# A graph network in one planned instruction order: the planner's costs for TensorE's switches, score tiles by pairs, and new aims

## The chip, the cores and the metric

The kernel runs on one NeuronCore of one Trainium2 chip. The metric is the device time of one execution in microseconds (us). The engines are TensorE (PE; its weight loads are shown as PEld), VectorE (DVE), ScalarE (ACT), GpSimd (POOL) and SyncE (SP). Each takes its own instructions in the order in which the program lists them.

## The reference, cut to what matters

There are 16 graphs (the batches) of N = 1024 nodes with D = 256 features and an integer adjacency matrix each. All of it is fp32. Layer 0 is attention with 8 heads of 32, masked by the adjacency; layer 1 is two graph attentions and a feed-forward network.

```
# layer 0, per batch
q, k, v = heads(x @ Wq), heads(x @ Wk), heads(x @ Wv)
e = einsum('hqd,hkd->hqk', q, k);  e = where(e >= 0, e, 0.2 * e)
h = softmax(where(adj > 0, e, NEG), axis=-1) @ v
y = layernorm(h, g1, b1)
x = layernorm(concat([y, x]) @ Wffn.T, g2, b2) + x
# layer 1, per batch
def gat(h, W, a):
    Wh = h @ W
    e = leaky_relu(Wh @ a[:F] + (Wh @ a[F:]).T, 0.2)
    return softmax(where(adj > 0, e, NEG), axis=1) @ Wh
h = layernorm(x + gat(gat(x, W1, a1), W2, a2), g_ln1, b_ln1)
x = layernorm(h + relu(h @ w_ff1 + b_ff1) @ w_ff2 + b_ff2, g_ln2, b_ln2)
```

## The kernel before

**The planner.** The whole program is one stream of instructions whose order is worked out when it is built. Each piece of work is a Python generator, called a thread here. Before it emits an instruction it yields `on(PE=..., ACT=..., DVE=..., POOL=..., SP=...)`, the cost in ns of that instruction on the engine or engines that could do it; it can also `take` and `give` a buffer of a pool, `wait` for an event, `fire` one, `start` another thread or set its `aim`, a due time. The class `Order` keeps a clock for every engine. Of all threads that could start within a window of 300 ns of the earliest, the one with the earliest aim goes next; where a thread names two engines, the one that ends first takes it. So a wrong cost does no harm to a result: it only puts instructions into another order. On the chip the engines follow the order as it stands and wait for each other by semaphores.

`HOP` and `TAIL` are delays from one engine to the next, `SWITCH` a price for a change between two kinds of products on TensorE. Operations that are marked `shared` (DVE with two SBUF inputs, and the multiplication on POOL) are kept from overlapping by `port`, the time at which the other engine may start.

**The work of a batch.** Scores are made transposed, one tile of 128 keys by all 1024 queries: two matmuls of 512 columns (`all_scores`, L605), 64 tiles in a batch, in PSUM tiles of two banks of which there are two. A tile then goes through `weights`: ACT copies 0.2 times the scores (L621), DVE takes the maximum of the two (L623, which frees the PSUM tile), ACT the exponential (L626), POOL multiplies by the mask (L630). `all_values` takes the tiles two by two: products with v, 32 columns wide and called narrow (L645), and products with a column of -1 that sum the weights; for half of them DVE first adds two tiles (`add_pair`, L675). A narrow tile is four products of 256 columns, each in its own quarter of the array. After a head, `after_head` takes out the sums (`ho`) and divides.

When all heads of a batch are done, `rest` runs for it beside the scores of the next: layer norm and the product with `Wffn` (`rows_pair`, L771, L774), rows of the graph layer (L803), two graph attentions (`attend`, L856 and L859 on DVE, eight tiles each; products L894 and L919), a feed-forward network (L959, L987), with transposes on TensorE (L366, L695, L839, L947) between. `project` prepares the batch after: transposes of x (L366), masks (L433), q and k (L486) and v (L518). These products share three PSUM banks, the pool `misc`.

**What sets the order.** The aims are shares of `SLOT`, 253 us, counted from a batch's first score: `AIM` for steady batches, `EARLY` for the first. `graph0`, `graph1` and `graph_step` give those of `attend`, `qk0`, `qk1` and `qk_step` those of the projections. A score tile is due at a fixed pace and can't start earlier than `lead` paces ahead of it:

```
due = t0 + (h * NT + t) / 2 * pace(b)
yield aim(due, AIM["lead"] * PACE)
yield take("scores")
ps = psum.tile([P, N], FT, tag="scores", name="ps_s")
yield on(PE=471)
```

Row statistics (`stats`) are two instructions on DVE per row tile and then a logarithm and an exponential on ACT (L349, L351), which the planner counts as 98 ns each.

Of the kernel before, what the change touches and what calls it, by code (L numbers as in the profile page):

```python
# [27 lines left out]
BIG = float(2**100)  # L28
# [6 lines left out]
class Order:  # L35
# [5 lines left out]
    HOP = dict(PE=53.0, ACT=35.0, DVE=36.0, POOL=80.0, SP=60.0)  # L41
    TAIL = dict(PE=163.0, ACT=103.0, DVE=84.0, POOL=42.0, SP=0.0)
    WINDOW = 300.0
    SWITCH = 93.0

    STRETCH = 3413.0
    WORK = 0.43

    def __init__(self, **pools):
        self.clock = defaultdict(float)  # L50
        self.port = 0.0
        self.transfers = 0.0
        self.narrow = False
        self.stretch, self.done, self.half = 0, 0.0, True
        self.pools = {k: [(0.0, i) for i in range(n)] for k, n in pools.items()}
        self.slot = {}
        self.queues = defaultdict(list)
        self.events = {}
        self.waiting = defaultdict(list)
        self.active = []  # L60
        self.made = 0
        self.now = 0.0
        self.busy = defaultdict(float)
# [73 lines left out]
    def run(self):  # L137
        while self.active:
            could = []
            for th in self.active:  # L140
                costs, shared, delay, narrow = th["op"]
                best = None
                for engine, cost in costs.items():
                    ready = th["ready"] + self.HOP[engine]
                    if th.get("last", ())[:2] == (engine, th["ready"]):
                        ready -= self.HOP[engine] + self.TAIL[engine]
                    t = asked = max(self.clock[engine], ready)
                    if shared and engine in ("DVE", "POOL"):
                        t = max(t, self.port)
                    if best is None or t + cost < best[0] + best[2]:  # L150
                        best = t, engine, cost, asked
                could.append((best, th))
            first = min(c[0][0] for c in could)
            (t, engine, cost, asked), th = min((c for c in could if c[0][0] <= first + self.WINDOW),
                                        key=lambda c: (c[1]["aim"], c[1]["no"]))
            if th["op"][1] and engine in ("DVE", "POOL"):

                before = [c for c in could if c[1]["op"][1] and c[0][1] in ("DVE", "POOL")
                          and c[0][1] != engine and c[0][3] < asked]
                if before:  # L160
                    (t, engine, cost, asked), th = min(before, key=lambda c: (c[1]["aim"], c[1]["no"]))
            costs, shared, delay, narrow = th["op"]
            self.active.remove(th)
            if engine == "PE":
                if narrow != self.narrow:
                    cost += self.SWITCH
                self.narrow = narrow
            end = self.clock[engine] = self.end(engine, t, cost)
            self.busy[engine] += cost
            if shared and engine in ("DVE", "POOL"):  # L170
                self.port = end
            self.now = t
            th["ready"] = end + self.TAIL[engine]
            th["last"] = engine, th["ready"]
            if delay:
                self.transfers = max(self.transfers, end + 1000) + 1450 * max(1, round(cost / 500))
                th["ready"] = max(end + delay, self.transfers + 1200)
                th["last"] = None, 0
            self.step(th, engine)
        stuck = {k: len(v) for k, v in list(self.waiting.items()) + list(self.queues.items()) if v}  # L180
        assert not stuck, f"threads that never end: {stuck}"


def on(shared=False, delay=0.0, narrow=False, **costs):
    return "on", (costs, shared, delay, narrow)


def pause(time):
# [11 lines left out]
def take(pool):  # L200
    return "take", pool
# [10 lines left out]
def aim(time, lead):  # L212
    return "aim", (time, lead)
# [17 lines left out]
def unshifted_path(  # L231
# [26 lines left out]
    PACE = SLOT / (H * NT // 2)  # L258


    AIM = dict(mask0=0.759, x=0.5882, x_step=0.0012, mask=0.7438, mask_step=0.0264, qk0=0.6333, qk1=0.7649,
               qk_step=0.0231, v0=0.863, v1=0.9566, v_step=0.0513, rows=-0.1328, rows_step=0.0338, first0=0.1095,
               first1=0.2264, graph0=0.0576, graph1=0.273, graph_step=0.0015, second=0.3518, second_step=0.0609,
               normed=0.8572, normed_step=0.058, ff_wait=(None, 0, 1, 0), ff=(0.6792, -0.0871, 0.5781, 0.4984),
               ff_step=0.0581, fast0=0.4431, fast1=0.9245, fast15=0.6119, lead=1.5024)

    EARLY = dict(x=0.87, x_step=0.0004, mask=0.7193, mask_step=0.0345, qk0=0.7893, qk1=0.9441, qk_step=0.0345,
                 v0=0.8496, v1=0.9733, v_step=0.0532, rows=-0.139, rows_step=-0.0236, first0=0.1365,
                 first1=-0.0311, graph0=-0.195, graph1=-0.027, graph_step=0, second=0.3474, second_step=0.0327,
                 normed=0.781, normed_step=0.02, ff_wait=(None, 0, 1, 0), ff=(0.633, 0.0209, 0.488, 0.493),  # L270
                 ff_step=0.0422)

    const = ctx.enter_context(tc.tile_pool(name="const", bufs=1))
# [8 lines left out]
    def share(b, name):  # L282
        return (EARLY if b < 2 else AIM)[name]

# [52 lines left out]
    def stats(srcs):  # L337

        n = len(srcs)
        mv = small.tile([P, n, 2], FT, name=f"mv{n}")  # L340
        for i, src in enumerate(srcs):
            st = small.tile([P, 6], FT, name="st")
            yield on(DVE=430)
            nc.vector.bn_stats(st, src)
            yield on(DVE=99)
            nc.vector.bn_aggr(mv[:, i, :], st)
        rs = small.tile([P, n], FT, name=f"rs{n}")
        yield on(ACT=98)
        nc.scalar.activation(rs, mv[:, :, 1], AF.Ln, bias=eps)  # L349
        yield on(ACT=98)  # L350
        nc.scalar.activation(rs, rs, AF.Exp, scale=-0.5)  # L351
        return mv, rs

# [231 lines left out]
    def pace(b):  # L585
        return PACE * {0: AIM["fast0"], 1: AIM["fast1"], B - 1: AIM["fast15"]}.get(b, 1.0)

    def all_scores():
        for b in range(B):
            yield wait(("stack", b, 0))  # L590
            t0 = begin[b] = work.now
            if b + 1 < B:
                yield start(project(b + 1, t0), t0)
            for h in range(H):
                yield wait(("stack", b, h))
                q, kk = stacks[b, h]
                for t in range(NT):
                    due = t0 + (h * NT + t) / 2 * pace(b)
                    yield aim(due, AIM["lead"] * PACE)
                    yield take("scores")  # L600
                    ps = psum.tile([P, N], FT, tag="scores", name="ps_s")
                    yield on(PE=471)
                    for nh in range(NH):
                        cols = slice(nh * HALF, (nh + 1) * HALF)
                        nc.tensor.matmul(ps[:, cols], kk[:, t * P:(t + 1) * P], q[:, cols], start=True, stop=True)  # L605
# [27 lines left out]
    def all_values():  # L633
        for b in range(B):
            for h in range(H):
# [13 lines left out]
                for d in range(0, NT, GV):  # L649
                    last, adds = d + GV == NT, d < ADDED * GV  # L650
                    for t in range(d, d + GV):
                        yield wait(("p", b, h, t))
                    if added:
                        yield wait(("p added", b, h, d - GV))
                    yield aim(begin[b] + (h * NT + d + 2) / 2 * pace(b), SLOT)
                    ps = [probs.pop((b, h, t)) for t in range(d, d + GV)]
                    for t, p in zip(range(d, d + GV), ps):
                        yield on(PE=430, narrow=True)
                        product(v[:, t, c:c + DH], p, 0, t == 0, False)
                        yield aim(begin[b], BIG)  # L660
                    if adds:
                        yield start(add_pair(b, h, d, ps), begin[b] + (h * NT + d + 2) / 2 * pace(b))
                    for p in added if adds else added + ps:
                        yield on(PE=430, narrow=True)
# [799 lines left out]
```

## Time and profile before

| | |
|---|---|
| median of 3 runs | 4434.45 us (4430.11 to 4434.94) |
| profiled execution | 4435.77 us, span 4433.9 us |
| busy, share of the span | PE 96%, PEld 70%, DVE 79%, ACT 68%, POOL 53% |
| mean clock granted to TensorE | 0.99 |
| scores, L605 | 2048 matmuls, 684.7 us busy |
| narrow products, L645 | 8192 and 6144 records, 559.2 and 407.9 us |
| maximum, L623 | 1024 on DVE, mean 1215 ns |
| mask, L630 | 1024 on POOL, mean 2332 ns |
| `attend`, L856 and L859 | 256 each on DVE, means 1446 and 1343 ns |
| logarithm, L349; exponential, L351 | 224 each on ACT, medians 296 and about 200 ns |

The span is the time from the first to the last instruction that the profiler saw. Busy times of TensorE overlap, since matmuls are pipelined; the distance from one start to the next says more. A number in square brackets in a timeline is idle time of that engine before the instruction, and the name behind it what ended it.

### The profile page before, as it was taken

What the parts mean: (1) busy time and instruction counts of PE and PEld (TensorE: products, weight loads), DVE (VectorE), ACT (ScalarE), POOL (GpSimd) and SP (SyncE); (2) the same over time, 40 slices, a digit from 0 to 9 for tenths busy, and PEclk for the clock granted to TensorE, in tenths of its full rate; (3) what the DMA queues carried; (4) which work ended last, traced back from release to release, by engine and by line L of the source; (5) the groups of instructions that cost most, each with busy time, mean ns of one, the idle gap of its engine ahead of it and who ended that gap; (6) DMA issues with size and microseconds to landing.
All of it is one profiled execution on the core that took longest, in us unless ns stands there. A gap on an engine that the chain in (4) does not pass through costs nothing.

```text
span 4433.9 us, 77232 instructions
## 1 busy us (share of the span) xinstructions
PE 4267.4 (96%) x30539; PEld 3082.5 (70%) x30539; DVE 3515.0 (79%) x5493; ACT 3004.8 (68%) x4488; POOL 2364.4 (53%) x1033
## 2 busy tenths in 40 slices
PE   8888999999999999999999999999999999999899
PEld 4455667677676776767777676776767777677687
DVE  6877878888788888888878788887788878788853
ACT  6656675676867667676676867667676676867632
POOL 5746464464736536473564736537464564736600
PEclk9999999999999999999999999999999999999999
DMA  5413223232222322222232222322323232221100
GB/s 181 124 53 87 74 72 87 70 93 70 87 79 70 93 67 83 83 83 82 65 95 73 86 79 70 94 67 77 84 81 88 63 96 74 86 79 41 34 20 20
DMA packets 156286, 344.86 MB, mean 78 GB/s; under 512 B 21750, under 2 KB 24332, under 8 KB 155916
## 3 DMA queue, kind: packets, MB, share of 16 engines
q1 hardware_dynamic: 112140, 260.13, 20.5%
q10 hardware_dynamic: 43776, 79.71, 6.3%
q8 instruction: 243, 3.98, 0.4%
q14 instruction: 127, 1.04, 0.1%
HBM read 239.09 MB, written 100.66 MB: 77 GB/s over the span
## 4 chain that ended last, share of the span: by engine, by line
PE 67%; DVE 28%; ACT 3%; issue 2%; POOL 0%; DMA 0%; ACTq 0%; SPq 0%; DVEq 0%; POOLq 0%
PE ps_a L645 15%; PE ps_s L605 10%; PE ps_m L894 9%; PE ps_m L919 8%; DVE att L856 7%; DVE att L859 6%; DVE p L623 5%; PE ps_m L959 4%; PE ps_m L486 4%; PE ps_m L987 3%; PE ps_m L771 3%; PE ps_m L803 2%; PE ps_m L774 2%; ACT p L621 2%; PE ps_m L366 1%
## 5 line engine op out<-in xcount | busy, mean ns | idle before, releaser
L630 POOL TENSOR_TENSOR p<-p,mask 128x1024 f32<-128x1024 f32 x1024 | 2363.6, 2332 | 1837.8 <-ACT p L626 1338.2
L623 DVE TENSOR_TENSOR p<-p,ps_s 128x1024 f32<-128x1024 f32 x1024 | 1220.1, 1215 | 344.5 <-ACT p L621 336.6
L626 ACT ACTIVATE p<-p 128x1024 f32<-128x1024 f32 x1024 | 1082.2, 1059 | 301.1 <-DVE p L623 256.4
L621 ACT ACTIVATE p<-ps_s 128x1024 f32<-128x1024 f32 x1006 | 996.0, 1020 | 198.2 <-PE ps_s L605 91.9
L605 PE MATMUL ps_s<-qs,ks 128*128 128x512 f32 x2048 | 684.7, 439 | 50.6 <-DVE p L623 46.6
L645 PE MATMUL ps_a<-p,v 128*32 128x256 f32 x8192 | 559.2, 388 | 12.2 <-POOL p L630 12.2
L605 PEld LDWEIGHTS ps_s<-qs,ks 128*128 128x128 f32 x2048 | 337.1, 190 | 276.2 <-issue 116.5
L894 PE MATMUL ps_m<-y,att 128*128 128x258 f32 x2048 | 484.6, 382 | 5.5 <-ACT y L864 1.9
L919 PE MATMUL ps_m<-y,att 128*128 128x256 f32 x2048 | 480.9, 381 | 1.8 <-ACT y L864 1.8
L959 PE MATMUL ps_m<-rT,wf 128*128 128x256 f32 x2048 | 472.6, 381 | 7.1 <-ACT z L324 2.4
L987 PE MATMUL ps_m<-wf,hid 128*128 128x256 f32 x2048 | 473.8, 380 | 1.3 <-ACT xT L324 1.1
L894 PEld LDWEIGHTS ps_m<-y,att 128*128 128x128 f32 x2048 | 386.4, 190 | 76.7 <-ACT hid L968 6.1
L645 PE MATMUL ps_a<-p,minus_ones 128*32 128x256 f32 x6144 | 407.9, 383 | 31.8 <-DVE p L675 31.5
L959 PEld LDWEIGHTS ps_m<-rT,wf 128*128 128x128 f32 x2048 | 379.6, 190 | 69.8 <-ACT hid L968 8.1
L987 PEld LDWEIGHTS ps_m<-wf,hid 128*128 128x128 f32 x2048 | 379.3, 190 | 59.1 <-issue 7.6
L919 PEld LDWEIGHTS ps_m<-y,att 128*128 128x128 f32 x2048 | 379.7, 190 | 55.8 <-ACT y L864 2.6
L645 PEld LDWEIGHTS ps_a<-p,v 128*32 128x32 f32 x8192 | 213.4, 109 | 288.7 <-issue 155.2
L675 DVE TENSOR_TENSOR p<-p 128x1024 f32<-128x1024 f32 x256 | 374.1, 1461 | 18.2 <-PE ps_a L645 16.8
L856 DVE SCALAR_TENSOR_TENSOR att<-first,second 128x1024 f32<-128x1024 f32 x256 | 370.1, 1446 | 13.5 <-ACT first L843 13.5
L859 DVE SCALAR_TENSOR_TENSOR att<-mask,att 128x1024 f32<-128x1024 fp8e4 x256 | 343.8, 1343 | 7.7
L645 PEld LDWEIGHTS ps_a<-p,minus_ones 128*32 128x32 f32 x6144 | 199.0, 111 | 172.4 <-DVE p L675 41.3
L864 ACT ACTIVATE y<-y,check 128x258 f32<-128x258 f32 x256 | 130.6, 510 | 247.6 <-DVE check L862 246.4
(106 smaller groups left out, 4427.8 us busy)
## 6 DMA issues: line engine op xcount, KB each, us to landing
qs<-qk_halves SPq DMA_DIRECT2D x256, 256.0 KB, 3.7
ks<-qk_halves SPq DMA_DIRECT2D x256, 256.0 KB, 5.1
adj_i<-in_adj_dram ACTq DMA_DIRECT2D x240, 256.0 KB, 3.2
qk_halves<-high SPq DMA_DIRECT2D x128, 256.0 KB, 2.5
qk_halves<-low SPq DMA_DIRECT2D x128, 256.0 KB, 2.9
xr<-in_x_dram ACTq DMA_DIRECT2D x64, 256.0 KB, 3.0
x_kept<-x SPq DMA_DIRECT2D x64, 256.0 KB, 2.1
x<-x_kept SPq DMA_DIRECT2D x64, 256.0 KB, 3.2
```

The costliest lines, as they stand in the source:

```text
L605: nc.tensor.matmul(ps[:, cols], kk[:, t * P:(t + 1) * P], q[:, cols], start=True, stop=True)
L621: nc.scalar.activation(p, ps, AF.Copy, scale=ALPHA)
L623: nc.vector.tensor_tensor(p, p, ps, op=OP.max)
L626: nc.scalar.activation(p, p, AF.Exp)
L630: nc.gpsimd.tensor_tensor(p, p, mask_of(b, t), op=OP.mult)
L645: nc.tensor.matmul(acc[i * DH:(i + 1) * DH, at:at + QN], w, p[:, i * QN:(i + 1) * QN], start=first, stop=last)
L856: nc.vector.scalar_tensor_tensor(e, first[:, 0, :], second[:, j:j + 1], first[:, 1, :], op0=OP.mult, op1=OP.max)
L859: nc.vector.scalar_tensor_tensor(e, mask_of(b, j), -1.0, e, op0=OP.mult, op1=OP.mult, accum_out=sums[:, j:j + 1])
L894: nc.tensor.matmul(pa[:, cols:cols + width], big[:, j, i * P:(i + 1) * P], rows[:, j, :width], start=(j == 0), stop=(j == NT - 1))
L919: nc.tensor.matmul(pa[:, i * D:(i + 1) * D], big[:, j, t * P:(t + 1) * P], y2[:, j, :D], start=(j == 0), stop=False)
L959: nc.tensor.matmul(pa[:, i * 2 * P:(i + 1) * 2 * P], wf1[:, dc, hc * P:(hc + 1) * P], rT[:, dc, :], start=(dc == 0), stop=(dc == DC - 1))
L987: nc.tensor.matmul(pa[:, i * D:(i + 1) * D], hid[hc // 2][:, hc % 2, i * P:(i + 1) * P], wf2[:, hc, :], start=(hc == 0), stop=False)
```

## The change

The planner's model gets new figures, and the order is worked out anew.

- The price of a switch on TensorE depends on what comes from and what goes to: `SWITCH` is a table over `narrow`, `single` (scores) and other products. A score tile costs 464 instead of 471.
- The shared port is kept for DVE and POOL apart: after a DVE operation POOL may start 54 ns before its end, after one on POOL DVE 130 ns before its end.
- The logarithm and the exponential of `stats` cost 318 and 105 ns.
- From batch 1 on, scores go by pairs of key tiles: at an even tile the thread takes both PSUM tiles of the pool, and the odd tile follows without a due time of its own.
- `AIM` and `EARLY` have new values.

The instructions themselves are the same but for the engine that takes a result out of PSUM, where the planner has the choice.

```
-    SWITCH = 93.0
+    SWITCH = {(None, "narrow"): 93.0, ("single", "narrow"): 93.0, ("narrow", None): 93.0,
+              ("narrow", "single"): 197.0, (None, "single"): 84.0}
...
-        self.port = 0.0
+        self.port = dict(DVE=0.0, POOL=0.0)
-        self.narrow = False
+        self.mode = None
...
                     if shared and engine in ("DVE", "POOL"):
-                        t = max(t, self.port)
+                        t = max(t, self.port[engine])
...
             if engine == "PE":
-                if narrow != self.narrow:
-                    cost += self.SWITCH
-                self.narrow = narrow
+                cost += self.SWITCH.get((self.mode, mode), 0.0)
+                self.mode = mode
...
             if shared and engine in ("DVE", "POOL"):
-                self.port = end
+                if engine == "DVE":
+                    self.port["POOL"] = end - 54.0
+                else:
+                    self.port["DVE"] = end - 130.0
...
-    AIM = dict(mask0=0.759, x=0.5882, x_step=0.0012, mask=0.7438, mask_step=0.0264, qk0=0.6333, qk1=0.7649,
-               qk_step=0.0231, v0=0.863, v1=0.9566, v_step=0.0513, rows=-0.1328, rows_step=0.0338, first0=0.1095,
-               first1=0.2264, graph0=0.0576, graph1=0.273, graph_step=0.0015, second=0.3518, second_step=0.0609,
-               normed=0.8572, normed_step=0.058, ff_wait=(None, 0, 1, 0), ff=(0.6792, -0.0871, 0.5781, 0.4984),
-               ff_step=0.0581, fast0=0.4431, fast1=0.9245, fast15=0.6119, lead=1.5024)
+    AIM = dict(mask0=0.7454, x=0.7836, x_step=0.0012, mask=0.7416, mask_step=0.0241, qk0=0.8169, qk1=0.7629,
+               qk_step=0.0234, v0=0.8897, v1=0.9566, v_step=0.0513, rows=-0.1328, rows_step=0.039, first0=0.1101,
+               first1=0.2264, graph0=-0.041, graph1=0.3629, graph_step=0.0128, second=0.3518, second_step=0.0609,
+               normed=0.8572, normed_step=0.058, ff_wait=(None, 0, 1, 0), ff=(0.6792, -0.0021, 0.5781, 0.4984),
+               ff_step=0.0549, fast0=0.4291, fast1=0.9756, fast15=0.6646, lead=1.5024)
...
-    EARLY = dict(x=0.87, x_step=0.0004, mask=0.7193, mask_step=0.0345, qk0=0.7893, qk1=0.9441, qk_step=0.0345,
+    EARLY = dict(x=0.9697, x_step=0.0004, mask=0.7306, mask_step=0.0331, qk0=0.7893, qk1=0.9441, qk_step=0.026,
...
-                 first1=-0.0311, graph0=-0.195, graph1=-0.027, graph_step=0, second=0.3474, second_step=0.0327,
+                 first1=-0.0311, graph0=-0.0903, graph1=-0.027, graph_step=0, second=0.3474, second_step=0.0327,
...
-        yield on(ACT=98)
+        yield on(ACT=318)
         nc.scalar.activation(rs, mv[:, :, 1], AF.Ln, bias=eps)
-        yield on(ACT=98)
+        yield on(ACT=105)
         nc.scalar.activation(rs, rs, AF.Exp, scale=-0.5)
...
-                    yield aim(due, AIM["lead"] * PACE)
-                    yield take("scores")
+                    if b == 0 or t % 2 == 0:
+                        yield aim(due, AIM["lead"] * PACE)
+                        for _ in range(2 if b else 1):
+                            yield take("scores")
+                    else:
+                        yield aim(t0, BIG)
                     ps = psum.tile([P, N], FT, tag="scores", name="ps_s")
-                    yield on(PE=471)
+                    yield on(PE=464, mode="single")
...
-                        yield on(PE=430, narrow=True)
+                        yield on(PE=430, mode="narrow")
```

More of the change, by code (lines that the diff above doesn't have):

```diff
@@ L140, in run @@
             for th in self.active:
-                costs, shared, delay, narrow = th["op"]
+                costs, shared, delay, mode = th["op"]
                 best = None
@@ L161, in run @@
                     (t, engine, cost, asked), th = min(before, key=lambda c: (c[1]["aim"], c[1]["no"]))
-            costs, shared, delay, narrow = th["op"]
+            costs, shared, delay, mode = th["op"]
             self.active.remove(th)
             if engine == "PE":
-                if narrow != self.narrow:
-                    cost += self.SWITCH
-                self.narrow = narrow
+                cost += self.SWITCH.get((self.mode, mode), 0.0)
+                self.mode = mode
             end = self.clock[engine] = self.end(engine, t, cost)
@@ L181, in run, with on @@
         assert not stuck, f"threads that never end: {stuck}"
-def on(shared=False, delay=0.0, narrow=False, **costs):
-    return "on", (costs, shared, delay, narrow)
+def on(shared=False, delay=0.0, mode=None, **costs):
+    return "on", (costs, shared, delay, mode)
 def pause(time):
@@ L258, in unshifted_path @@
     PACE = SLOT / (H * NT // 2)
-    AIM = dict(mask0=0.759, x=0.5882, x_step=0.0012, mask=0.7438, mask_step=0.0264, qk0=0.6333, qk1=0.7649,
-               qk_step=0.0231, v0=0.863, v1=0.9566, v_step=0.0513, rows=-0.1328, rows_step=0.0338, first0=0.1095,
-               first1=0.2264, graph0=0.0576, graph1=0.273, graph_step=0.0015, second=0.3518, second_step=0.0609,
-               normed=0.8572, normed_step=0.058, ff_wait=(None, 0, 1, 0), ff=(0.6792, -0.0871, 0.5781, 0.4984),
-               ff_step=0.0581, fast0=0.4431, fast1=0.9245, fast15=0.6119, lead=1.5024)
-    EARLY = dict(x=0.87, x_step=0.0004, mask=0.7193, mask_step=0.0345, qk0=0.7893, qk1=0.9441, qk_step=0.0345,
-                 v0=0.8496, v1=0.9733, v_step=0.0532, rows=-0.139, rows_step=-0.0236, first0=0.1365,
-                 first1=-0.0311, graph0=-0.195, graph1=-0.027, graph_step=0, second=0.3474, second_step=0.0327,
-                 normed=0.781, normed_step=0.02, ff_wait=(None, 0, 1, 0), ff=(0.633, 0.0209, 0.488, 0.493),
+    AIM = dict(mask0=0.7454, x=0.7836, x_step=0.0012, mask=0.7416, mask_step=0.0241, qk0=0.8169, qk1=0.7629,
[4 more added lines that the diff above has]
+    EARLY = dict(x=0.9697, x_step=0.0004, mask=0.7306, mask_step=0.0331, qk0=0.7893, qk1=0.9441, qk_step=0.026,
+                 v0=0.8496, v1=0.9733, v_step=0.0532, rows=-0.1833, rows_step=-0.0236, first0=0.1365,
+                 first1=-0.0311, graph0=-0.0903, graph1=-0.027, graph_step=0, second=0.3474, second_step=0.0327,
+                 normed=0.781, normed_step=0.02, ff_wait=(None, 0, 1, 0), ff=(0.6698, 0.0209, 0.488, 0.4266),
                  ff_step=0.0422)
@@ L663, in all_values @@
                     for p in added if adds else added + ps:
-                        yield on(PE=430, narrow=True)
+                        yield on(PE=430, mode="narrow")
                         product(minus_ones, p, QN, False, last and p is ps[-1])
```

## The prediction

> **What bounds the kernel now.** I read the page from the top, then asked where TensorE waits, then compared stretches of one batch.
>
> ```profile
> span 4433.9 us, 77232 instructions
> ...
> PE 4267.4 (96%) x30539; PEld 3082.5 (70%) x30539; DVE 3515.0 (79%) x5493; ACT 3004.8 (68%) x4488; POOL 2364.4 (53%) x1033
> ...
> PEclk9999999999999999999999999999999999999999
> ```
>
> TensorE is the bound, the clock is full nearly everywhere, and a busy TensorE is not one at its peak. So I measured its work by the distances from start to start in its timeline, taking the undisturbed ones as the cost. A 256-wide fp32 pass takes 0.216 us, a score tile (two matmuls) 0.464, a tile of narrow products (L645, eight records) 0.431. A narrow run costs 0.231 more than its tiles, in and out together, and a score tile right behind it 0.106 more again; behind other products a score tile costs nothing extra (0.680 from a 256-wide start to the instruction after the tile, less 0.216, is 0.464). With 515 narrow runs, 331 of them followed by scores, this makes 4124.6 us of work. The other 309 us of the span are stalls. From the first score of a batch to that of the next it is 266.8 us in the steady batches (5 to 14): 257.1 of work, 9.7 of stall.
>
> ```profile
> 1955.28 1.07 PE L645 MATMUL ps_a<-p,v 128*32 128x256 f32 x16
> 1956.17 0.61 PE L645 MATMUL ps_a<-p,minus_ones 128*32 128x256 f32 x8
> 1956.71 1.20 PE L605 MATMUL ps_s<-qs,ks 128*128 128x512 f32 x4
> 1957.75 1.90 PE L894 MATMUL ps_m<-y,att 128*128 128x258 f32 x8
> ...
> 1880.44 1.99 PE L987 MATMUL ps_m<-wf,hid 128*128 128x256 f32 x8
> 1882.90 0.70 PE L605 MATMUL ps_s<-qs,ks 128*128 128x512 f32 x2 [0.47 <-DVE p L623]
> 1883.94 0.73 PE L605 MATMUL ps_s<-qs,ks 128*128 128x512 f32 x2 [0.34 <-DVE p L623]
> ```
>
> The first four lines are a clean stretch: a pair of score tiles takes 1.04 us, 0.93 and the step out of narrow mode. In the last three, 2.46 us lie between the start of eight passes, worth 1.73, and the tile behind them, and the two tiles stand 1.04 us apart instead of 0.46: both wait for VectorE to free a score bank.
>
> ```profile
> 1815.00:1915.00 100.00, 97.36 (x654) 74.22 (x652) 86.20 (x161) 66.64 (x124) 34.19 (x16) 1.00 0.21 61
> 1915.00:2081.00 166.00, 165.03 (x1254) 116.70 (x1250) 131.02 (x181) 122.50 (x158) 111.44 (x49) 1.00 0.32 91
> ```
>
> The columns after the length are busy us of PE, PEld, DVE, ACT and POOL. Most of the stall lies in the first 100 us of a batch, where DVE is busiest. By what follows it, a steady batch stalls 4.9 us before or within score tiles, 4.8 among other products, 0.3 in narrow runs.
>
> ```profile
> 1894.46 1.25 DVE L856 SCALAR_TENSOR_TENSOR att<-first,second 128x1024 f32<-128x1024 f32 x1
> 1895.74 1.22 DVE L859 SCALAR_TENSOR_TENSOR att<-mask,att 128x1024 f32<-128x1024 fp8e4 x1
> ...
> 1828.75 0.30 ACT L349 ACTIVATE rs<-mv,eps 128x2 f32<-128x2 f32 x1
> 1829.07 0.20 ACT L351 ACTIVATE rs<-rs 128x2 f32<-128x2 f32 x1
> 1829.18 1.01 ACT L621 ACTIVATE p<-ps_s 128x1024 f32<-128x1024 f32 x1
> ...
> PE ps_s L605 <- DVE p L623: 46.6, 84, 1.9
> PE ps_a L645 <- DVE p L675: 31.5, 5, 9.5
> ```
>
> DVE runs `attend` (L856, L859) seven or eight tiles in a row, 2.6 us each; the score stalls sit around these two blocks, and behind one of them a product waits up to 9.5 us (last line, from TensorE's waits). The ACT lines show the pair Ln, Exp at a pitch of 0.32 and 0.11 us, where the planner has 98 ns each.
>
> **What the Trainium skill says.** "TensorEngine Tiling (Array Packing)", Key Properties: a change of tiling mode drains TensorE. The trace agrees: other to narrow and narrow to other are 0.093 us longer each. "TensorE: Matmul & The Clock Gate", the section on the 32x32 sub-arrays: ACT and DVE are strict FIFO; so a maximum (L623) behind eight `attend` tiles waits for all of them, as here. "SBUF — State Buffer", section "SBUF: two separate sides": DVE with two SBUF inputs and GpSimd lock each other out of a shared port for a whole instruction. The trace agrees: L856 is 1.25 us alone and 3.13 beside L630 at 1887.06. The new port rule lets the second start slightly before the first ends.
>
> **The change, part by part.** No product, size or buffer changes; the built programs have the same number of matmuls, POOL operations and DMA issues. What changes is the order on every queue and which engine evacuates: 32 instructions go from ACT to DVE, 28 of them `ho` (0.58 us on ACT, 0.69 on DVE), some 1.3 us more DVE in a batch. I price that at nothing: DVE has 49 us free in a steady batch, and ACT loses as much.
>
> *Switches.* Counted in both orders and priced as above: narrow runs go from 32 to 35 in a steady batch (+3 x 0.231 = +0.69 us), score runs behind narrow ones from 20 to 14 (-6 x 0.106 = -0.64). Over the kernel it is 515 to 547 and 331 to 252: +7.4 - 8.4 = **-1 us**. The model's 84 ns for other-to-score, which the trace doesn't show, makes the planner pay in narrow runs for nothing.
>
> *Loads.* The new aims move the q and k projections, and with them the DMAs on SP, as well as the issues of `xr` and masks on ACT. By TensorE's work the last projection stands 87 us ahead of the next batch's first score, where it was 81; writing and reading back take 2.9 and 5.1 us from issue to landing (rows of the DMA issues), and the queues are 20 and 6% busy. Cost nothing; without that cover it would be those 8 us a batch.
>
> *Pairs.* From batch 1 on both score banks must be free before a pair is issued, and pairs go from 350 to 485. In a steady batch the TensorE work between the ends of tile k-2 and the start of tile k is at least 4.1 us, where it was 2.4. What a pair needs: 0.46 and 0.2 to ACT, two copies (L621) at 0.90, the second maximum 1.13, hops 0.3, 3.9 us from its start, 3.0 in the measure above. So pairs alone cause no wait. Yet large slack did not prevent stalls before: tiles with 30 us of slack waited 0.4 to 0.6 us, behind the `attend` blocks.
>
> *Blocks.* The longest DVE work between two maxima falls from 26.7 and 25.1 us to 19.0 and 14.9 (sums of pitches in the DVE order), to 0.65 of it. I scale the score stall with that: 4.9 to 3.2, **-1.7** a batch (bounds: 0 and -4.9).
>
> *ACT and port figures.* 14 groups of Ln and Exp in a batch, each counted 0.227 us too short (0.423 new, 0.196 old), put ACT 3.2 us behind plan in a batch. Work placed to be just in time came late. Of the 4.8 us among other products I take a third, **-1.6** (bounds: +1, since new neighbours bring new misses, and -3.2). What is late next: the transposes behind `y` and `hT` (L366), whose chain through statistics stays as long.
>
> So a steady batch gains 3.3 us; with batches 4 to 14, eleven: **-36**. *Batches 1 to 3 and 15.* Batch 1 has stalls of 9.9 us at 274.9 and 383.8, behind blocks of 27.9 and 19.4 us that become 18.2 and 17.5: half of the 9.7 and 1.9 that go, -6. Batches 2 and 3 as the steady ones, -7. Batch 15: 9.9 us at 4160.9 behind a block that goes from 17.8 to 11.7, -3. Together **-16** (bounds: +10 and -35; their aims moved most, and the trace has no other order to compare). Batch 0 keeps single tiles: 0.
>
> The sum is -1 - 36 - 16 = -53 against the profiled execution's 4435.8 us (span 4433.9, 1.9 around it), thus **4382 us**; the median shown, 4434.45, is 1.3 lower.
>
> **Rivals.** *Nearly all stalls behind DVE go*: 4.9 + 2.4 in eleven batches is 80, with 25 at the ends: 4330. For it: the middle of each batch shows no stall, so the order can be that good. Against it: `attend` is still 20 us of DVE twice a batch. *The stalls only move*: TensorE reaches the next late operand sooner, and the 4.8 us grow by what the scores save; only a part of the ends is won: 4430. For it: DVE is busy 86 of 100 us where it matters, and gets more. *Slower: pairs crowd the evacuations.* Two copies and two maxima stand together on ACT and DVE, so one of the three `misc` banks is freed later and the product for it stalls everything behind it on TensorE. A batch has 32 pairs; from 3.3/32 = 0.10 us per pair this eats the gain, and at 0.20 us, with the ends' gain lost too, it is 36 us slower: 4472. For it: ACT evacuations of 0.47 to 0.58 us already wait behind L621 and L626. Against it: the clean middle is made of pairs already. That the pairing is not in effect is excluded: the new order shows 485 pairs.
>
> **How the numbers follow.** Some 8.9 us (0.2%) is what a measurement of this kernel can tell from no change. Moderate gain 0.52 (own range 4355 to 4420), nearly all 0.18, stalls move 0.16, slower 0.14. Of the third, more than half is within 0.2%. Faster 0.77, same 0.09, slower 0.14. The range 4335 to 4445 leaves out the worse half of the slower case and the tail of the best.
>
> **What would show it.** A steady batch near 263.5 us instead of 266.8; TensorE's wait of L612 for the maximum (now L630) down by a third; no 9.9 us wait behind L682; TensorE's work still near 4124 us. A batch as long as before with fewer score waits would prove the second rival, longer waits of products for ACT or DVE the third. Steady batches below 261 us would mean that I undersized the blocks.

## The result, and the profile after

The new kernel takes **4402.17 us** (median of 6 runs, 4396.82 to 4403.73); the kernel before takes 4434.41 us beside it (4430.11 to 4435.19). The ratio is 0.9926, with an interval of 0.9913 to 0.9938: 0.74% faster, 32 us. The profiled execution took 4397.53 us; its span is 38.2 us shorter.

The head of the page of the new kernel:

```profile
span 4395.7 us, 77297 instructions
...
PE 4246.0 (97%) x30539; PEld 3077.3 (70%) x30539; DVE 3543.5 (81%) x5525; ACT 2979.7 (68%) x4456; POOL 2418.1 (55%) x1033
...
PEclk9999999999999999999999999999999999999999
```

The matmuls are as many as before, at the same clock. TensorE is busy 21 us less although it does the same products: its overlapping busy time is no measure of work. Priced from start to start, as in the prediction, its work is 4123.6 us after 4124.6. So the gain is stall that went. The first score of each batch gives the stretches (us):

| stretch | before | after | change |
|---|---|---|---|
| to the first score | 38.6 | 37.1 | -1.5 |
| batches 0 to 3 | 977.5 | 967.0 | -10.5 |
| batches 4 to 14 | 2933.4 | 2906.7 | -26.7 |
| batch 15, to the last score | 246.6 | 252.1 | +5.5 |
| after the last score | 237.8 | 232.8 | -5.0 |

A steady batch now takes 264.3 us instead of 266.8, with 7.2 of stall instead of 9.7. Where in the batch the stall lies depends on how it is counted. The prediction says that its split (4.9, 4.8, 0.3) goes by what follows the stall. Its figures come out of the trace in another way: a stall behind a score tile or a narrow run, in front of another product, is in them counted with the tile or the run ahead of it. Counted by the matmul that comes late, the split is different. All these are estimates from the distances from start to start, good to some 0.3 us:

| stall of a steady batch, us | before, as the prediction counts | after, same count | before, by the matmul that comes late | after, same count |
|---|---|---|---|---|
| score tiles | 4.9 | 2.4 | 3.9 | 0.6 |
| other products | 4.8 | 3.7 | 5.5 | 6.3 |
| narrow products | 0.3 | 1.1 | 0.3 | 0.3 |

Below, the split is by the matmul that comes late. Scores have lost 3.3 us of stall, and other products have gained 0.8.

The two stretches of one batch of the new kernel (columns as in the prediction: length, then busy us of PE, PEld, DVE, ACT and POOL):

```profile
1795.00:1895.00 100.00, 98.23 (x654) 75.78 (x656) 84.93 (x169) 67.70 (x122) 35.04 (x16) 1.00 0.20 57
1895.00:2059.00 164.00, 163.04 (x1253) 115.02 (x1246) 135.39 (x176) 118.52 (x158) 114.31 (x49) 1.00 0.33 95
```

With the same 654 products, TensorE is idle 1.8 us in the first stretch where it was 2.6; the loss stays in the part where `attend` runs, and is smaller. TensorE's waits from 1300 to 3600 us, some nine steady batches, name it (what it waited for: us in total, times, longest). Before:

```profile
PE ps_s L605 <- DVE p L623: 12.4, 35, 0.5
PE ps_m L366 <- DVE y L360: 4.7, 9, 0.5
PE ps_m L771 <- ACT mask L437: 3.6, 9, 0.4
PE ps_m L959 <- ACT z L324: 2.1, 9, 0.2
PE ps_m L366 <- ACT hT L385: 1.5, 9, 0.2
PE ps_m L695 <- DVE rT L383: 1.5, 8, 0.2
```

After:

```profile
PE ps_m L369 <- DVE rT L386: 6.7, 8, 0.9
PE ps_m L966 <- ACT z L327: 6.4, 9, 0.7
PE ps_m L994 <- DVE hn L709: 5.9, 9, 0.7
PE ps_m L846 <- ACT first L850: 2.2, 9, 0.2
PE ps_m L436 <- DVE rT L386: 0.8, 5, 0.2
PE ps_s L612 <- DVE p L630: 0.7, 1, 0.7
PE ps_m L846 <- DVE low L494: 0.3, 1, 0.3
```

The waits of scores for the maximum have all but gone from the steady part (12.4 to 0.7 us). Those of other products have grown from 13.4 to 22.3 us; the three longest of them come about once a batch each. In the new list every one is a wait for a bank of `misc`: the instruction named behind the arrow takes a result out of such a bank and is no operand of the product. Before, that for `y` was a wait for an operand; the other four, 8.7 us, were for a bank too. This view counts only idle time that it can put down to a semaphore, so it shows less than the distances do. Over the whole span of the new kernel:

```profile
PE ps_s L612 <- DVE p L630: 35.3, 36, 4.9
PE ps_a L652 <- DVE p L682: 25.2, 11, 9.5
```

Of the 35.3 us, 0.7 lie in the window above; before it was 12.4 of 46.6. Outside the window the score waits are as large as ever, 34.6 after 34.2. And the wait behind `add_pair` (now L682) is still there: 25.2 us after 31.5.

The chain of work that ended last says the same from the other side, by engine. Before, then after:

```profile
PE 67%; DVE 28%; ACT 3%; issue 2%; POOL 0%; DMA 0%; ACTq 0%; SPq 0%; DVEq 0%; POOLq 0%
```
```profile
PE 81%; DVE 14%; ACT 3%; issue 2%; POOL 0%; DMA 0%; ACTq 0%; SPq 0%; DVEq 0%; POOLq 0%
```

DVE's share of the chain has halved, while its busy time has grown by 28 us.

### The profile page after: what moved, and what is told of

The parts are those of the page before. It is cut to its first block, busy times and chain, and to the rows that moved or that the text cites. A ratio compares the mean times of both kernels' runs of the same rounds, so it can differ in the third digit from the quotient of the medians.

```text
span 4395.7 us, 77297 instructions
## 1 busy us (share of the span) xinstructions
PE 4246.0 (97%) x30539; PEld 3077.3 (70%) x30539; DVE 3543.5 (81%) x5525; ACT 2979.7 (68%) x4456; POOL 2418.1 (55%) x1033
## 4 chain that ended last, share of the span: by engine, by line
PE 81%; DVE 14%; ACT 3%; issue 2%; POOL 0%; DMA 0%; ACTq 0%; SPq 0%; DVEq 0%; POOLq 0%
PE ps_a L652 16%; PE ps_m L901 10%; PE ps_s L612 9%; PE ps_m L926 9%; PE ps_m L994 8%; PE ps_m L966 8%; DVE p L630 4%; PE ps_m L489 4%; PE ps_m L810 3%; DVE att L863 3%; PE ps_m L778 3%; PE ps_m L781 2%; DVE att L866 2%; PE ps_m L369 2%; PE ps_m L521 2%
## 5 line engine op out<-in xcount | busy, mean ns | idle before, releaser
L637 POOL TENSOR_TENSOR p<-p,mask 128x1024 f32<-128x1024 f32 x1024 | 2417.3, 2377 | 1752.1 <-ACT p L633 1401.4
L612 PE MATMUL ps_s<-qs,ks 128*128 128x512 f32 x2048 | 639.1, 430 | 35.5 <-DVE p L630 35.3
L612 PEld LDWEIGHTS ps_s<-qs,ks 128*128 128x128 f32 x2048 | 350.0, 190 | 213.5 <-issue 68.0
L966 PE MATMUL ps_m<-rT,wf 128*128 128x256 f32 x2048 | 472.7, 381 | 13.2 <-ACT z L327 7.3
L966 PEld LDWEIGHTS ps_m<-rT,wf 128*128 128x128 f32 x2048 | 380.6, 190 | 81.8 <-issue 11.0
L652 PE MATMUL ps_a<-p,minus_ones 128*32 128x256 f32 x6144 | 408.7, 384 | 25.2 <-DVE p L682 25.2
L682 DVE TENSOR_TENSOR p<-p 128x1024 f32<-128x1024 f32 x256 | 385.4, 1506 | 25.7 <-PE ps_a L652 25.6
L863 DVE SCALAR_TENSOR_TENSOR att<-first,second 128x1024 f32<-128x1024 f32 x256 | 393.7, 1538 | 4.5 <-ACT first L850 4.5
L866 DVE SCALAR_TENSOR_TENSOR att<-mask,att 128x1024 f32<-128x1024 fp8e4 x256 | 353.0, 1379 | 5.9
```

The source lines that it names most:

```text
L637: nc.gpsimd.tensor_tensor(p, p, mask_of(b, t), op=OP.mult)
L652: nc.tensor.matmul(acc[i * DH:(i + 1) * DH, at:at + QN], w, p[:, i * QN:(i + 1) * QN], start=first, stop=last)
L863: nc.vector.scalar_tensor_tensor(e, first[:, 0, :], second[:, j:j + 1], first[:, 1, :], op0=OP.mult, op1=OP.max)
L866: nc.vector.scalar_tensor_tensor(e, mask_of(b, j), -1.0, e, op0=OP.mult, op1=OP.mult, accum_out=sums[:, j:j + 1])
L966: nc.tensor.matmul(pa[:, i * 2 * P:(i + 1) * 2 * P], wf1[:, dc, hc * P:(hc + 1) * P], rT[:, dc, :], start=(dc == 0), stop=(dc == DC - 1))
```

## Experiments

### One part alone: the planner draws another order each time

The theory was that parts of the change could be priced one by one. The rival: any new figure gives another order, and orders differ more than parts do. Four kernels test it: in two the cost of a narrow tile is one ns higher, in the order before and in the new one, and two make one part of the change alone.

```
b_431, a_431:   -  yield on(PE=430, ...)    +  yield on(PE=431, ...)     (both places in all_values)
b_pairs:        the kernel before, with the new loop of `all_scores` (pairs from batch 1 on)
b_newaims:      the kernel before, with the new AIM and EARLY
```

> The kernel before with one planner figure moved by 1 ns (a narrow tile 430 to 431), which gives another order and no better model. Theory 'costs' (the gain comes from figures that fit the chip): within 8 us of 4434. Theory 'draw' (any newly planned order falls somewhere in a wide spread, and the changed kernel's is a good one): off by more than 15 us, up or down. TensorE's own work by the count of switches is 2.7 us more than before (4129.2 to 4126.5).

> The changed kernel with the same 1 ns (430 to 431). 'Costs': within 8 us of 4402. 'Draw': the spread again, most likely slower, 4415 to 4440, since the changed kernel's order was one of many. Work by the count 4122.4, 3 us less than the changed kernel.

> The kernel before with the scores by pairs alone, old costs and old aims. Theory 'pairs': at least half of the gain, below 4418. 'Costs' and 'aims': 4425 to 4440, no gain. 'Draw': anything from 4405 to 4450.

> The kernel before with the new AIM and EARLY alone, old costs and single tiles. Theory 'aims': below 4418. 'Costs' and 'pairs': about 4434. If the aims only fit the new model: slower, 4440 to 4460.

| kernel | us | against before (4430.31 there) | TensorE's work, us |
|---|---|---|---|
| b_431 | 4486.39 | 1.0124 [1.0107, 1.0141] | 4127.3 |
| a_431 | 4521.71 | 1.0203 [1.0186, 1.0220] | 4120.5 |
| b_pairs | 4519.19 | 1.0200 [1.0183, 1.0217] | 4124.6 |
| b_newaims | 4524.81 | 1.0213 [1.0196, 1.0230] | 4125.8 |

The expectation that one ns would cost little failed: it costs 56 us in the old order, and puts the new one some 120 us above its own time. TensorE's work is 4120 to 4127 us in all six orders (these four and the two kernels of the change), so nearly all of it is stall. The slowdown is more than the expectations had for a mere draw, too: they went to 4440 us for a_431, 4450 for b_pairs and, for aims that only fit the new model, 4460 for b_newaims. What sets the two kernels of the change apart is that their batches repeat: from batch 5 on the lengths agree to a few tenths of a us, but for one of the new kernel's batches that stalls 1.3 us more. In b_431 steady batches take 261 to 281 us, in a_431 266 to 295. TensorE's waits in a_431:

```profile
PE ps_m L994 <- DVE hn L709: 58.6, 4, 14.9
```

Four waits of up to 14.9 us each, for a bank of `misc` that the division of a head's output (`hn`) frees: together they cost more than the whole change saves. Which due time brought them about was not traced. Pairs alone (+2.0%) and aims alone (+2.1%) say nothing of their part in the change; costs, pairs and aims are one chosen set. Which of them made the better order possible stays open.

### The same order, other durations: logarithm and exponential

From here on the order is kept to the instruction and one duration is changed on the chip, in the order before (b_) and in the new one (a_). If the lateness of ACT's statistics was what the old order lost, taking it away must help the old order and not the new one.

```
+        lnv = small.tile([P, 4], FT, name="lnv", bufs=1)[:, :n]
-        nc.scalar.activation(rs, mv[:, :, 1], AF.Ln, bias=eps)
+        nc.scalar.activation(lnv, mv[:, :, 1], AF.Ln, bias=eps)
-        nc.scalar.activation(rs, rs, AF.Exp, scale=-0.5)
+        nc.scalar.activation(rs, mv[:, :, 1], AF.Exp, scale=-0.5)
```

> The order of the kernel before, to the instruction; on ACT the exponential of the row statistics reads the variance instead of the logarithm's result, so that it need not wait for it. The reciprocal root is left out by this (rows are scaled by another number). Logarithm and exponential then take about 0.20 us together, what the old planner counts, instead of 0.43: 224 x 0.23 = 51 us less of ACT. Theory 'costs' (the old order stalls because ACT comes later than planned): the 4.8 us of stall a steady batch among other products fall to 3.7 or less, 10 to 25 us of the whole. Theory 'order' (the stalls are those of the order's own shape around the attend blocks): within 6 us of before. 'Draw' says nothing here, the order is the same.

> The same edit in the changed kernel's order, which was planned with 0.42 us for the two. 'Costs': less than a third of what it brings before, since this order has reckoned with the time: 0 to 7 us. 'Order': within 6 us of 4402.

ACT's timeline in b_stats:

```profile
1827.82 0.30 ACT L350 ACTIVATE lnv<-mv,eps 128x2 f32<-128x2 f32 x1
1828.01 0.20 ACT L352 ACTIVATE rs<-mv 128x2 f32<-128x2 f32 x1
1828.10 1.02 ACT L622 ACTIVATE p<-ps_s 128x1024 f32<-128x1024 f32 x1
```

The exponential starts 0.19 us after the logarithm, not 0.32: the pair takes 0.28 us instead of 0.43. Two thirds of the 0.227 us by which the old figures were short are gone. Yet the kernel gains little: b_stats takes 4425.49 us, ratio 0.9987 [0.9978, 0.9996], with a span 3.3 us shorter and a steady stall of 9.5 instead of 9.7. a_stats takes 4397.22 us, 0.9921 [0.9903, 0.9939] of the kernel before; its span is 1.6 us shorter than that of the new kernel. If 0.227 us per group had cost 1.6 us a batch, 0.15 should have brought some 1.1; it brought 0.1 to 0.2. Of the two theories, 'costs' (10 to 25 us in the old order) has failed, and 'order' holds.

### The same order: a shorter attend

`attend` makes its first operation (L856) with one input instead of two SBUF inputs and a column; the second is unchanged.

```
-        nc.vector.scalar_tensor_tensor(e, first[:, 0, :], second[:, j:j + 1], first[:, 1, :],
-                                       op0=OP.mult, op1=OP.max)
+        nc.vector.tensor_scalar(e, first[:, 0, :], 1.0, None, op0=OP.mult)
```

> The order of the kernel before, to the instruction; the first of the two DVE operations of attend becomes a multiplication by one of one half of its input (the weights of the graph attention are left out by this), about 0.6 us instead of 1.30, so that a block of eight is some 5 us shorter. If the score stalls (4.9 us in a steady batch) come from the blocks: down to 2.5 or less, and with the stalls of 9.9 us behind the products shortened by about 5 each, 35 to 60 us of the whole. If they come from the spacing of the tiles: under 12 us.

> The same edit in the changed kernel's order. If blocks cause its score stalls (2.4 us in a steady batch) too: down to about 1.2, 15 to 35 us of the whole, less than in the order before, so that the two come closer than 32 us. If the gain of the new order lies elsewhere: the distance of 32 us stays.

The operation falls from a mean of 1446 ns to 858. b_att takes 4391.14 us, 0.9904 [0.9887, 0.9922]: 43 us less. a_att takes 4368.57, 0.9855 [0.9837, 0.9873]: 34 us less than the new kernel. TensorE's waits in b_att, in the window of nine batches:

```profile
PE ps_s L605 <- DVE p L623: 4.6, 18, 0.3
PE ps_m L366 <- DVE y L360: 4.2, 8, 0.5
```

The waits of scores fall from 12.4 to 4.6 us without any other order. A steady batch of b_att stalls 7.9 us, of which 2.7 ahead of or within score tiles instead of 3.9; batches 1 and 2 stall 46.3 and 16.9 us instead of 59.2 and 22.2. The whole gain lies in the range that was expected; the score stall was to be halved and fell by a third. So DVE's time around `attend` does hold up the scores. The new order gains from it too (steady stall 7.2 to 6.0), and 23 of the 32 us between the orders remain: shorter DVE work alone does not make them equal.

### The same order: how long POOL holds the port

`attend`'s first operation has two SBUF inputs, as `add_pair` has. The Trainium skill ("SBUF — State Buffer", section "Who interferes with whom") says that such an operation contends with a GpSimd instruction that reads SBUF, and not with one that only writes. That allows two experiments. In the first, POOL multiplies half of each tile. In the second, it also fills the other half with ones, twice, so that a tile keeps POOL as long as before and only half of that time reads SBUF.

```
b_pool, a_pool:
-        nc.gpsimd.tensor_tensor(p, p, mask_of(b, t), op=OP.mult)
+        nc.gpsimd.tensor_tensor(p[:, :HALF], p[:, :HALF], mask_of(b, t)[:, :HALF], op=OP.mult)
b_lock, a_lock, besides, ahead of it:
+        nc.gpsimd.memset(p[:, HALF:], 1.0)
+        nc.gpsimd.memset(p[:, HALF:], 1.0)
```

> The order of the kernel before, to the instruction; POOL multiplies only the first 512 of 1024 columns of a tile by the mask (the other half stays unmasked, which is left out by this), about 1.2 us instead of 2.33, so that it holds the port that it shares with DVE half as long and weights are ready 1.1 us earlier. If what is left of the stalls comes from DVE operations that wait for POOL (attend beside POOL takes 3.1 us instead of 1.25): the score stall of a steady batch falls from 4.9 to under 3, 25 to 50 us of the whole. If the chains of transposes and evacuations alone set it: under 10 us.

> The same edit in the changed kernel's order. If the new port figures of the planner already place DVE and POOL well: less than half of what it brings in the order before, under 20 us. If the port holds both orders alike: the same, and the distance of 32 us stays.

> The order of the kernel before, with POOL's time per tile kept at about 2.2 us but half of it spent on two writes that read nothing (memset of the other 512 columns to one) ahead of the half multiplication; half of the weights are ones by this, left out of the computation. It tells the two readings of b_pool apart. If the stalls come from DVE operations that wait while POOL reads and writes SBUF: the steady batch goes from 266.8 to about 264 us as in b_pool. If they came from weights being ready late: it stays at 266 to 267. If memset holds the port as well: no change either, and DVE's attend stays at a mean near 1.45 us.

> The same edit in the changed kernel's order. Port reading: the steady batch stays between 263.9 and 264.3 us, so that both orders take the same time per batch; the whole is 10 to 30 us faster, from the first and last batches. Late-weights reading: no change at all.

The sums of weights leave the bounds that the kernel tests in all four, and the program then runs `general_path`, a second computation, behind the first. Their whole times (17,713.54, 17,699.13, 17,702.58 and 17,688.86 us; 4.00, 4.00, 4.00 and 3.99 times the kernel before) say nothing here. What is read is the first computation, up to its last score, one profile each. The rows of b_att and a_att stand beside for comparison; how long DVE is busy is the mean of ten steady batches:

| | steady batch, us | its stall: scores, other, narrow | DVE busy in it, us | last score, us |
|---|---|---|---|---|
| before | 266.8 | 3.9, 5.5, 0.3 | 218 | 4196.1 |
| b_att | 265.0 | 2.7, 5.1, 0.1 | 209 | 4153.3 |
| b_pool | 263.9 | 2.1, 4.6, 0.1 | 202 | 4136.5 |
| b_lock | 263.8 | 2.2, 4.3, 0.1 | 203 | 4133.4 |
| after | 264.3 | 0.6, 6.3, 0.3 | 220 | 4162.9 |
| a_att | 263.3 | 0.4, 5.6, 0.1 | 209 | 4133.9 |
| a_pool | 263.9 | 0.3, 6.3, 0.1 | 207 | 4130.1 |
| a_lock | 263.1 | 0.3, 5.5, 0.1 | 209 | 4137.0 |

The groups of `attend`'s first operation before and in b_pool, then those of b_lock (count, then busy us and mean ns):

```profile
L856 DVE SCALAR_TENSOR_TENSOR att<-first,second 128x1024 f32<-128x1024 f32 x256 | 370.1, 1446 | 13.5 <-ACT first L843 13.5
L856 DVE SCALAR_TENSOR_TENSOR att<-first,second 128x1024 f32<-128x1024 f32 x256 | 328.6, 1284 | 17.8 <-ACT first L843 17.8
...
L632 POOL TENSOR_TENSOR p<-p,mask 128x512 f32<-128x512 f32 x1024 | 1256.2, 1227 | 0.0
L630 POOL MEMSET p<- 128x512 f32 x1024 | 546.2, 533 | 1799.6 <-ACT p L626 1794.2 <-PE ps_a L647 3.0
L858 DVE SCALAR_TENSOR_TENSOR att<-first,second 128x1024 f32<-128x1024 f32 x256 | 328.9, 1285 | 18.9 <-ACT first L845 18.9
```

Two memsets and half a multiplication make 2.29 us of POOL per tile, against 2332 ns before: the weights come no earlier. `attend`'s operation falls from 1446 to 1285 ns, near the 1.25 us that it takes alone, and takes as long as without memsets (1284 in b_pool), so the memsets do not hold it up. And the old order loses its handicap: its batch falls to 263.8 us. The new order gains less, 0.4 and 1.2 us a batch. So the distance in a steady batch, 2.5 us, falls to none with half the multiplication and to 0.7 with the memsets, and at the last score the distance between the orders is 6.4 us with half the multiplication and -3.6 with the memsets, where it was 33.2. TensorE's waits in b_lock, in the window:

```profile
PE ps_s L605 <- DVE p L623: 4.3, 14, 0.4
```

It is the same fall as in b_att, though POOL is nearly as busy as ever. One place of the order shows the way from the port to a score. The two score tiles of the old order that the prediction shows at 1882.90 and 1883.94 us wait for maxima (L623) that stand behind this on DVE:

```profile
1876.11 2.44 DVE L1000 SCALAR_TENSOR_TENSOR z<-z,rs,bl 128x256 f32<-128x256 f32 x1
1879.04 2.59 DVE L856 SCALAR_TENSOR_TENSOR att<-first,second 128x1024 f32<-128x1024 f32 x1
1881.55 2.34 DVE L623 TENSOR_TENSOR p<-p,ps_s 128x1024 f32<-128x1024 f32 x2
```

POOL multiplies two tiles meanwhile:

```profile
1876.12 4.43 POOL L630 TENSOR_TENSOR p<-p,mask 128x1024 f32<-128x1024 f32 x2 [1.49 <-ACT p L626]
```

The same instructions in b_lock, and the two score tiles, now without a wait:

```profile
1840.18 0.48 DVE L1002 SCALAR_TENSOR_TENSOR z<-z,rs,bl 128x256 f32<-128x256 f32 x1
1842.65 1.28 DVE L858 SCALAR_TENSOR_TENSOR att<-first,second 128x1024 f32<-128x1024 f32 x1 [0.55 <-ACT first L845]
1843.85 2.34 DVE L623 TENSOR_TENSOR p<-p,ps_s 128x1024 f32<-128x1024 f32 x2
...
1846.16 1.27 PE L605 MATMUL ps_s<-qs,ks 128*128 128x512 f32 x4
```

The profiled first computation of one kernel stands for each line of the table, and the times of one and the same kernel differ by up to 14 us (4425.5 to 4439.2 for the kernel before, in 15 runs on one chip), so neither 6.4 nor -3.6 can be told from no distance. Against the expectations: b_pool gains 60 us up to the last score, more than the 25 to 50 expected, and a_pool 33, more than half of that, where either less than 20 or the same was expected; b_lock's batch of 263.8 fits the port reading; a_lock gains 26 us as that reading had it, but its batch is shorter than the 263.9 to 264.3 expected.

So in the old order DVE operations stood behind POOL's multiplication at the shared port, some 15 us of DVE's time in a steady batch (218 to 203), and with these waits shortened most of the distance is gone. It is not POOL's speed: b_pool, where the weights come a microsecond earlier, gains no more than b_lock. Three things qualify this. The waits are not those of `attend` alone: by the means of the groups it has about 4 of the 15 us, and `add_pair`, the rows `y` and the rows `z` about 3 to 4 each. Of the 3.1 us that b_lock gains in a batch, 1.7 come from scores and 1.2 from other products, so the scores' own distance does not close: 2.2 stay against 0.3. And a rival is left untested: any DVE time that goes may do as much. In the old order a us of DVE's time is worth about 0.2 us of a batch, in b_att (1.8 for 9) as in b_lock (3.1 for 15); in the new one it is worth about 0.1 (1.0 for 11, and 1.2 for 10). b_lock closes more of the distance than b_att at least in part because it frees more of DVE in the old order and no more in the new one.

The new order does not do it by keeping the two apart. The same group in the new kernel:

```profile
L863 DVE SCALAR_TENSOR_TENSOR att<-first,second 128x1024 f32<-128x1024 f32 x256 | 393.7, 1538 | 4.5 <-ACT first L850 4.5
```

At 1538 ns it meets POOL more than before (1446). Its maxima stand where the delay reaches few scores. DVE's timeline in the new kernel, in the block of a steady batch:

```profile
1868.54 1.20 DVE L630 TENSOR_TENSOR p<-p,ps_s 128x1024 f32<-128x1024 f32 x1
1870.21 1.51 DVE L863 SCALAR_TENSOR_TENSOR att<-first,second 128x1024 f32<-128x1024 f32 x1
1872.20 2.60 DVE L866 SCALAR_TENSOR_TENSOR att<-mask,att 128x1024 f32<-128x1024 fp8e4 x1
```

The second operation takes 2.60 us here instead of 1.22, and no score waits behind it: TensorE runs 24 matmuls of L966 from 1871.66 us and other products after them, and five more tiles of `attend` are through before DVE comes to the next maximum, at 1890.45. Whether the new port figures, the pairs or the aims brought that about was not tried in a way that could tell, since each alone draws another order.

## Why the prediction was right or wrong

The direction held, and 4402 lies within the range, 20 us above the number. The number owes part of this to luck: in the steady batches two terms were far off, in opposite directions. By the prediction's steps:

- **Switches, -1 us: right.** TensorE's work went from 4124.6 to 4123.6 us.
- **Pairs alone cause no wait: held for the scores in the steady part.** Scores wait 0.7 us for the maximum in nine batches made of pairs. The third rival, in which pairs crowd the evacuations, named longer waits of products for ACT or DVE as its sign. They did grow, from 13.4 to 22.3 us in the nine batches, and those for a bank of `misc` from 8.7 to 22.3. That is about 1 us a batch, too little to eat the gain. Whether the pairs cause it stays open.
- **Blocks of attend, -1.7 a batch: right in place, half the size.** The stall of scores fell by 3.3, from 3.9 to 0.6. The scaling by block length knew DVE's order only. b_att shows that DVE's time in the blocks matters; b_lock shows that waits at POOL's port are part of that time, and that with fewer of them the old order takes nearly as long per batch as the new one with the same edit. The prediction quoted the 3.13 us of one such wait and gave it no term.
- **ACT figures, -1.6 a batch: wrong.** The stall of other products did not fall but rose by 0.8. The fall by 1.1 in the prediction's own count comes from stalls that moved behind score tiles and narrow runs. b_stats removes two thirds of the lateness and gains 0.1 to 0.2 us, so lateness on ACT was not what the old order lost. What does shorten the stall of other products is DVE: by 1.2 in b_lock, where the wait for `y` (4.7 us in nine batches before) is gone from the list.
- **What is late next: half right.** The prediction named transposes behind `y` and `hT`. Late now are those behind `rT`, and products behind `z` and `hn`. Of the second rival, that the stalls only move, this much is true: a quarter of what the scores gained was lost again. All in all it is 2.5 us a batch in place of 3.3, a batch of 264.3 instead of 263.5. Over batches 4 to 14 it is 27 us instead of 36. Batch 4, counted as steady, gained next to nothing in stall (10.3 to 9.9); it is 2.7 us shorter because less work falls into it.
- **The ends, -16: too large.** To the first score and in batches 0 to 3 it is 12 us less, half a us more for batch 15 and the rest: 11.5 in all. Of the stall, batches 0 to 4 show 54.4, 59.2, 22.2, 12.7 and 10.3 before, 52.3, 55.5, 13.3, 16.5 and 9.9 after. The step that failed is the 9.9 us behind `add_pair`, which was to be halved or more in batches 1 and 15. From TensorE's timeline of the new kernel:

```profile
297.57 1.08 PE L652 MATMUL ps_a<-p,minus_ones 128*32 128x256 f32 x8 [9.47 <-DVE p L682]
...
390.32 1.08 PE L652 MATMUL ps_a<-p,minus_ones 128*32 128x256 f32 x8 [8.02 <-DVE p L682]
...
4111.41 1.50 PE L652 MATMUL ps_a<-p,minus_ones 128*32 128x256 f32 x24 [1.67 <-DVE p L682]
4117.83 0.91 PE L612 MATMUL ps_s<-qs,ks 128*128 128x512 f32 x2 [4.92 <-DVE p L630]
4122.35 2.35 PE L612 MATMUL ps_s<-qs,ks 128*128 128x512 f32 x4 [2.16 <-DVE p L630]
```

Both waits of batch 1 are there, at 297.57 and 390.32 us, 9.47 and 8.02 long, behind blocks a third and a tenth shorter. The one of batch 15 has split: 1.67 in the narrow run and 7.1 before the scores behind it. Here the second rival, stalls that only move, is the true account. In batch 1 DVE runs the last five tiles of `attend` from 283.08 to 296.2 us without a break, and `add_pair` is queued behind them, while TensorE comes to the product at 288. So the wait is what is left of the block when TensorE arrives, about the same in both orders, and not a share of the block's length.

Together 26.7 and 11.5 are the span's 38.2, the switches included. The wait of scores for the maximum fell over the whole span by a quarter (46.6 to 35.3 us), all of it in the steady part, where a third was forecast.

## What to carry to other kernels

Split a bound engine's time into work and stall by the distances between starts; if the work is the same in every order, only stalls are to be won, and the price of a part is the wait that it ends. Put each stall down to the instruction that comes late, and hold the split against the list of waits: counted with the neighbour ahead, the same stalls told another story here. A part of a planner's change can't be priced by planning without it, for one ns gives another order: keep the order to the instruction and change a duration on the chip, in the order before and in the one after, and see whether the distance between them closes. When a block of operations makes others late, look at how long its members take beside the other user of their port before scaling by its length.

## What the runs showed of the hardware

- A DVE operation with two SBUF inputs that takes 1285 ns on average beside POOL memsets and half multiplications takes 1446 to 1538 beside full multiplications. Memsets of 533 ns do not hold it up (1284 ns without them), as the page cited above says.
- An activation that reads what the one ahead of it wrote starts 0.32 us after it instead of 0.19, at two elements a partition, behind an instruction of 0.30 us: it does not overlap the one ahead, which the independent one does by about 0.1 us.
